# A two-layer graph convolution on one core: x loaded up front, row statistics on ScalarE, degree counting in pairs of edges, edge lists turned last

## The chip, the core and the metric

The kernel runs on one core of one Trainium2 chip. The core has five engines that run side by side, each through its own instruction list in order: PE (matrix products), DVE (VectorE), ACT (ScalarE), POOL (GpSimd) and SP (SyncE, which here only issues DMA transfers). Sixteen DMA engines move data between HBM and the on-chip memory SBUF. PE writes its products to PSUM, which DVE and ACT read. The metric is device time in microseconds (us) of one execution; the time of a kernel is the median of several runs.

## The reference

The input is x with 6250 nodes of 512 numbers, and 100000 edges (src, dst), sorted by dst. First each row of x is normalised and clipped at zero, then two Chebyshev graph convolutions run over it, with a layer norm and a leaky ReLU between them, and x is added at the end:

```python
h = jnp.maximum(_layernorm(x, axis=-1), 0.0)
deg = jax.ops.segment_sum(jnp.ones((src.shape[0],)), src, num_segments=n)
dinv = jnp.where(deg > 0, jax.lax.rsqrt(jnp.maximum(deg, 1.0)), 0.0)
norm = -dinv[src] * dinv[dst]
prop = lambda h: jax.ops.segment_sum(h[src] * norm[:, None], dst, num_segments=n)
h = h @ W1_0 + prop(h) @ W1_1 + b1
h = leaky_relu(layer_norm(h, gamma, beta))
out = x + h @ W2_0 + prop(h) @ W2_1 + b2
```

`deg` counts how often a node occurs in src. The factor `dinv[src]` can be put on the rows of a table before they are gathered, and `-dinv[dst]` on the sums.

## The kernel before

Nodes are cut into NB = 49 blocks of 128 (the last has 106), edges into NC = 782 chunks of 128. The kernel has a preparation and then `usual_path`, a loop over 2 layers by 49 blocks.

**Preparation** (`gnn_kernel`, L91 to L246), in the order of the code:

- Loads: `src_i`, the sources laid out 125 by 800 (L125); `dst_c` and `src_c`, the lists by chunks (L132 to L139), all on SP; four weight matrices and four vectors on ACT's queue (L142, L144). POOL makes number patterns (`diff`, `iota_r`), DVE makes the identity `ident` (L150).
- Turn of the edge lists (L157 to L169): PE transposes the 7 pieces of each list; the destinations stay in PSUM as `dl`, the sources are copied by ACT to `sidx`, the index list of the gathers.
- Degree count (L172 to L208): each source number is split into a low part (7 bits, `s_lo`) and a high part (`s_hi`, 0 to 48). In 50 rounds of GJ = 16 columns DVE compares the low parts with 0 to 127 (`lo`, L193) and the high parts with 0 to 48 (`hi`, L195), which gives one-hot rows in bf16; PE multiplies them, 16 products of 128 by 49 a round (L198), and sums them all in one PSUM tile `deg`. Then `dinv`, `ndinv` and `sdinv` are computed from it (L202 to L208).
- First table (L211 to L244): in 13 groups of GB = 4 blocks, three buffers deep, SP loads x (L219), DVE takes mean and variance of each row (L228, L229), ACT the square root (L231), DVE the scales (L234 to L238), ACT `relu(x*scale + bias)` with `dinv` multiplied in (L241), and SP stores the group to the table `tab[0]` in HBM (L243). The per-row scale and bias without `dinv` stay in `rs_all` and `nb_all` for the loop.

**The loop.** Each chunk's 128 source rows are fetched from the table by one indirect DMA on POOL (L272) into a ring of R = 44 buffers `zr`. The first gather waits for the whole table and for `sidx`. For each block DVE builds selection matrices `sel` (L324) from `dl`, PE multiplies them with the gathered rows (L335), in four strips of 32 output rows, ACT scales the sum to `agg` (L338), PE transposes it (L279) and multiplies it with one weight (L396). `own` (L283) loads the block's own rows of x again (L290), normalises them (L293), transposes them, and `start_products` (L302, its products at L304) multiplies them with the other weight. `finish` (L341) ends the block. PE and POOL follow the code's order exactly; the other engines are ordered by the scheduler. Memory of the preparation is given back at L246, and the loop's buffers take it over.

Of the kernel before, what the change touches and what calls it, by code (L numbers as in the profile page):

```python
# [8 lines left out]
F32 = mybir.dt.float32  # L9
BF = mybir.dt.bfloat16  # L10
I32 = mybir.dt.int32
AF = mybir.ActivationFunctionType
OP = mybir.AluOpType
# [5 lines left out]
P = 128  # L19
EPS = 1e-5  # L20
SLOPE = 0.01
# [7 lines left out]
def parts(r):  # L29

    return [(lo, hi) for lo, hi in ((0, r - r % 16), (r - r % 16, r)) if lo < hi]
# [16 lines left out]
def gnn_kernel(  # L48
# [27 lines left out]
    nc = tc.nc  # L76
    N, D = x.shape
    E = src.shape[0]
    NB = -(-N // P)
    EP = 125  # L80
    EJ = E // EP
# [7 lines left out]
    rows = [min(P, N - i * P) for i in range(NB)]  # L89
# [4 lines left out]
    def dup(ap, n):  # L94

        return bass.AP(tensor=ap.tensor, offset=ap.offset, ap=[[0, n], [1, ap.shape[0]]])

    tab = [dram.tile([NB * P, D], F32, name=f"tab{i}") for i in range(2)]
    h_tab = dram.tile([NB * P, D], F32, name="h_tab")

    ident = const.tile([P, P], F32, name="ident")
    iota_r = const.tile([P, P], F32, name="iota_r")
    ones = const.tile([P, P], F32, name="ones")
    eps = const.tile([P, 1], F32, name="eps")
    dinv = const.tile([P, NB], F32, name="dinv")
    ndinv = const.tile([P, NB], F32, name="ndinv")
    sdinv = const.tile([P, NB], F32, name="sdinv")
    rs_all = const.tile([P, NB], F32, name="rs_all")
    nb_all = const.tile([P, NB], F32, name="nb_all")
# [5 lines left out]
    n_seen = const.tile([P, NQ * NB], F32, name="n_seen")  # L115
# [6 lines left out]
    edges = ctx.enter_context(ExitStack())  # L122
    ep = edges.enter_context(tc.tile_pool(name="edges", bufs=1))
    src_i = ep.tile([EP, EJ], I32, name="src_i")
    nc.sync.dma_start(src_i, src.rearrange("(p j) -> p j", j=EJ))  # L125

    FG = NC // P - (E % (P * P) == 0)
    chunks = []
    for ids, fill, name in ((dst, NO_NODE, "dst_c"), (src, 0, "src_c")):
        t = ep.tile([P, NG, P], I32, name=name)  # L130
        nc.vector.memset(t[:, FG:, :], fill)
        nc.sync.dma_start(t[:, :FG, :], ids[: FG * P * P].rearrange("(g c e) -> c g e", c=P, e=P))  # L132
        whole = E // P - FG * P
        if whole:
            nc.sync.dma_start(t[:whole, FG, :],
                              ids[FG * P * P : (E // P) * P].rearrange("(c e) -> c e", e=P))
        if TAIL:
            nc.sync.dma_start(t[whole : whole + 1, FG, :TAIL],
                              ids[E - TAIL :].rearrange("(c e) -> c e", c=1))  # L139
        chunks.append(t)  # L140
    for t, w in zip(w_sb, (W1_1, W1_0, W2_1, W2_0)):
        nc.scalar.dma_start(t, w.rearrange("(k p) d -> p k d", p=P))  # L142
    for t, v in ((bias1, b1), (bias2, b2), (gam, gamma), (bet, beta)):
        nc.scalar.dma_start(t, dup(v, P))  # L144

    nc.gpsimd.iota(diff, pattern=[[1, P]], base=0, channel_multiplier=-1,
                   allow_small_or_imprecise_dtypes=True)
    nc.gpsimd.iota(iota_r, pattern=[[1, P]], base=0, channel_multiplier=0,
                   allow_small_or_imprecise_dtypes=True)
    nc.vector.tensor_single_scalar(ident, diff, 0.0, op=OP.is_equal)  # L150
    nc.vector.memset(ones, 1.0)
    nc.vector.memset(eps, EPS)

    nc.vector.memset(n_seen, 0.0)


    with tc.tile_pool(name="turn", bufs=1) as wp, tc.tile_pool(  # L157
        name="turn_ps", bufs=2, space=bass.MemoryType.PSUM
    ) as wps:
        for t, res in zip(chunks, (dl, sidx)):  # L160
            f = wp.tile([P, NG, P], F32, name="f", bufs=2)
            nc.vector.tensor_copy(f, t)
            for g in range(NG):
                if res is dl:
                    nc.tensor.transpose(dl[:, g * P : (g + 1) * P], f[:, g, :], ident)
                else:
                    fT = wps.tile([P, P], F32, name="fT")
                    nc.tensor.transpose(fT, f[:, g, :], ident)
                    nc.scalar.activation(sidx[:, g * P : (g + 1) * P], fT, AF.Copy)  # L169


    GJ = 16  # L172
    assert EJ % GJ == 0
    with tc.tile_pool(name="deg", bufs=1) as dp, tc.tile_pool(name="onehot", bufs=3) as ohp, tc.tile_pool(
        name="deg_ps", bufs=1, space=bass.MemoryType.PSUM
    ) as dps:
        iota_g = dp.tile([P, P, GJ], BF, name="iota_g")
        nc.gpsimd.iota(iota_g, pattern=[[1, P], [0, GJ]], base=0, channel_multiplier=0,
                       allow_small_or_imprecise_dtypes=True)
        half_i = dp.tile([EP, EJ], I32, name="half_i")  # L180
        s_lo = dp.tile([EP, EJ], BF, name="s_lo")
        s_hi = dp.tile([EP, EJ], BF, name="s_hi")
        nc.vector.tensor_single_scalar(half_i, src_i, P - 1, op=OP.bitwise_and)
        nc.vector.tensor_copy(s_lo, half_i)
        half_i2 = dp.tile([EP, EJ], I32, name="half_i2")
        nc.vector.tensor_single_scalar(half_i2, src_i, 7, op=OP.arith_shift_right)
        nc.vector.tensor_copy(s_hi, half_i2)
        deg = dps.tile([P, NB], F32, name="deg")
        for g in range(EJ // GJ):
            cols = slice(g * GJ, (g + 1) * GJ)  # L190
            lo = ohp.tile([EP, P, GJ], BF, name="lo")
            hi = ohp.tile([EP, NB, GJ], BF, name="hi")
            nc.vector.tensor_tensor(lo, s_lo[:, None, cols].to_broadcast([EP, P, GJ]),  # L193
                                    iota_g[:EP], op=OP.is_equal)
            nc.vector.tensor_tensor(hi, s_hi[:, None, cols].to_broadcast([EP, NB, GJ]),  # L195
                                    iota_g[:EP, :NB, :], op=OP.is_equal)
            for j in range(GJ):
                nc.tensor.matmul(deg, lo[:, :, j], hi[:, :, j], start=(g == 0 and j == 0),  # L198
                                 stop=(g == EJ // GJ - 1 and j == GJ - 1))
        root = dp.tile([P, NB], F32, name="root")  # L200
        some = dp.tile([P, NB], F32, name="some")
        nc.vector.tensor_scalar_max(root, deg, 1.0)  # L202
        nc.vector.tensor_single_scalar(some, deg, 0.0, op=OP.is_gt)
        nc.scalar.activation(root, root, AF.Sqrt)
        nc.vector.reciprocal(root, root)
        nc.vector.tensor_mul(dinv, root, some)
        nc.vector.tensor_scalar_mul(ndinv, dinv, -1.0)
        nc.vector.tensor_scalar_mul(sdinv, dinv, SLOPE)  # L208


    GB = 4  # L211
    with tc.tile_pool(name="t0", bufs=3) as pool:
        for i0 in range(0, NB, GB):
            g = [i for i in range(i0, min(NB, i0 + GB))]
            n = len(g)
            xt = pool.tile([P, GB, D], F32, name="xg")
            full = sum(rows[i] == P for i in g)
            if full:
                nc.sync.dma_start(xt[:, :full, :],  # L219
                                  x[i0 * P : (i0 + full) * P, :].rearrange("(i p) d -> p i d", p=P))  # L220
            if full < n:
                nc.vector.memset(xt[:, full:, :], 0.0)
                for lo, hi in parts(rows[g[-1]]):
                    nc.sync.dma_start(xt[lo:hi, full, :], x[g[-1] * P + lo : g[-1] * P + hi, :])
            st = pool.tile([P, GB, 6], F32, name="st")
            mv = pool.tile([P, GB, 2], F32, name="mv")
            for j in range(n):
                nc.vector.bn_stats(st[:, j, :], xt[:, j, :])  # L228
                nc.vector.bn_aggr(mv[:, j, :], st[:, j, :])  # L229
            sd = pool.tile([P, GB], F32, name="sd")  # L230
            nc.scalar.activation(sd[:, :n], mv[:, :n, 1], AF.Sqrt, bias=eps)  # L231
            rs = rs_all[:, i0 : i0 + n]
            nb = nb_all[:, i0 : i0 + n]
            nc.vector.reciprocal(rs, sd[:, :n])  # L234
            nc.vector.scalar_tensor_tensor(nb, mv[:, :n, 0], -1.0, rs, op0=OP.mult, op1=OP.mult)
            sc = pool.tile([P, 2, GB], F32, name="sc")
            nc.vector.tensor_mul(sc[:, 0, :n], rs, dinv[:, i0 : i0 + n])
            nc.vector.tensor_mul(sc[:, 1, :n], nb, dinv[:, i0 : i0 + n])  # L238
            t0 = pool.tile([P, GB, D], F32, name="t0")
            for j in range(n):  # L240
                nc.scalar.activation(t0[:, j, :], xt[:, j, :], AF.Relu, bias=sc[:, 1, j : j + 1],  # L241
                                     scale=sc[:, 0, j : j + 1])
            nc.sync.dma_start(tab[0][i0 * P : (i0 + n) * P, :].rearrange("(i p) d -> p i d", p=P),  # L243
                              t0[:, :n, :])  # L244

    edges.close()  # L246
    unseen = const.tile([1, 1], I32, name="unseen")
# [475 lines left out]
```

## Time and profile before

| what | us |
|---|---|
| median of 9 runs | 2750.56 |
| lowest and highest of them | 2728.08, 2762.71 |
| the profiled execution: its time, its span | 2739.88, 2738.0 |
| degree count, first compare to last product (L193 to L198) | 26.2 to 108.7 |
| loads of x for the table, first issue | 111.7 |
| last store to the table, issue | 193.1 |
| first gather | 197.5 |
| first and last `agg` of layer 1 | 271.7, 1493.4 |
| first gather, first `agg` of layer 2 | 1507.1, 1576.3 |

The profile's first part gives each engine's busy time, its share of the span, and its number of instructions:

```profile
PE 2148.9 (78%) x11848; PEld 817.0 (30%) x11848; DVE 653.8 (24%) x971; ACT 376.6 (14%) x672; POOL 1485.8 (54%) x1571
```

These shares are averages over stages that have nothing in common. In the first 200 us POOL gathers nothing, and from 127 to 201 us PE does little or nothing. A stage has to be read by itself, and for this the trace is cut into windows of time. A product of fp32 operands with 512 columns shows as two records on PE, so that 60 records of L335 are 30 products.

### The profile page before, as it was taken

Reading aid. Unit: us, or ns where it says so; the run is one execution under the profiler, and the core shown is the slowest. Engines: PE = TensorE matmul, PEld = TensorE weight load, DVE = VectorE, ACT = ScalarE, POOL = GpSimd, SP = SyncE. Lnnn points to the kernel's source line nnn. Section 1 sums busy time; section 2 is a strip of 40 time slices with the busy share of each in tenths; the row PEclk is TensorE's granted clock in tenths of the full one; section 3 lists DMA queues with packets and bytes.
Section 4 is the critical chain, followed back from the end, with each engine's and each line's share of the span. In section 5 each row is a group of like instructions: output and inputs, shape, how many; then the busy total and the mean of one; then the engine's idle time right before and its main releaser. Section 6 shows DMA issues by size and latency. Waiting matters only on the chain.

```text
span 2738.0 us, 29493 instructions
## 1 busy us (share of the span) xinstructions
PE 2148.9 (78%) x11848; PEld 817.0 (30%) x11848; DVE 653.8 (24%) x971; ACT 376.6 (14%) x672; POOL 1485.8 (54%) x1571
## 2 busy tenths in 40 slices
PE   6703888787878888787888388899888888879877
PEld 6600333232323322222333033332223222323332
DVE  7740322222222222222223011111111111111111
ACT  0240212111111212111222000000000000000000
POOL 0006666555555555645562666666666566555662
PEclk9955999999989999999999689999999999899999
DMA  3286676656666666756673667777776677666772
GB/s 103 99 310 186 207 211 197 192 170 196 190 182 180 185 196 181 207 155 187 191 209 123 195 198 214 206 211 212 210 208 206 185 211 211 190 184 200 214 212 89
DMA packets 184958, 521.13 MB, mean 190 GB/s; under 512 B 30379, under 2 KB 31941, under 8 KB 184810
## 3 DMA queue, kind: packets, MB, share of 16 engines
q0 software_dynamic: 125120, 410.09, 51.9%
q1 hardware_dynamic: 57002, 103.80, 11.2%
q10 hardware_dynamic: 2688, 5.24, 0.6%
q8 instruction: 95, 1.56, 0.2%
q14 instruction: 53, 0.43, 0.1%
HBM read 467.68 MB, written 51.34 MB: 190 GB/s over the span
## 4 chain that ended last, share of the span: by engine, by line
another core or an unknown queue 38%; PE 30%; DVE 12%; issue 9%; ACT 3%; DMA 0%; POOL 0%; ACTq 0%; DVEq 0%; SPq 0%; POOLq 0%
PE u_ps L396 13%; PE ps L335 10%; PE u_ps L304 4%; DVE sel L324 3%; PE aT_ps L279 2%; DVE aT L392 2%; DVE u_ps L358 1%; DVE u_ps L350 1%; DVE st L353 1%; DVE u_ps L360 1%; PE hT_ps L279 1%; DVE g L369 1%; ACT g L368 1%; ACT agg L338 1%
## 5 line engine op out<-in xcount | busy, mean ns | idle before, releaser
L272 POOL DMA_INDIRECT zr<-tab,sidx x1564 | 1482.7, 948 | 1184.7 <-PE ps L335 492.9
L335 PE MATMUL ps<-zr,sel 128*32 128x512 f32 x8680 | 1125.0, 597 | 148.5 <-DMA zr<-tab,sidx 89.6
L335 PEld LDWEIGHTS ps<-zr,sel 128*32 128x32 f32 x8680 | 319.5, 110 | 880.1 <-issue 833.5
L304 PE MATMUL u_ps<-w,hT 128*128 128x512 f32 x784 | 455.9, 710 | 17.0 <-issue 13.9
L396 PE MATMUL u_ps<-w,aT 128*128 128x512 f32 x784 | 398.6, 655 | 86.0 <-DVE aT L392 84.5
L324 DVE TENSOR_TENSOR sel<-dl,node 128x1536 f32<-128x1536 f32 (+5 forms) x110 | 160.9, 1472 | 1230.3 <-remote 1125.9
L279 PE MATMUL aT_ps<-ident,agg 128*128 128x128 f32 x392 | 78.4, 333 | 292.0 <-ACT agg L338 204.9
L396 PEld LDWEIGHTS u_ps<-w,aT 128*128 128x128 f32 x784 | 161.2, 213 | 344.2 <-issue 190.1
L338 ACT ACTIVATE agg<-ps,ndinv 128x512 f32<-128x512 f32 x98 | 67.4, 687 | 1302.9 <-remote 1173.5
L304 PEld LDWEIGHTS u_ps<-w,hT 128*128 128x128 f32 x784 | 157.3, 222 | 221.3 <-issue 217.6
L279 PEld LDWEIGHTS aT_ps<-ident,agg 128*128 128x128 f32 x392 | 50.2, 164 | 374.6 <-ACT agg L338 258.8
L297 ACT ACTIVATE hT<-hT_ps 128x512 f32<-128x512 f32 x98 | 58.5, 597 | 695.3 <-PE hT_ps L279 491.2
L392 DVE COPY aT<-aT_ps 128x512 f32<-128x512 f32 x98 | 67.8, 692 | 195.4 <-remote 148.0
L345 DVE TENSOR_TENSOR u_ps<-u_ps,bias 128x512 f32<-128x512 f32 x48 | 33.6, 700 | 253.4 <-PE u_ps L396 102.0
L350 DVE TENSOR_TENSOR u_ps<-u_ps,bias 128x512 f32<-128x512 f32 x49 | 34.3, 700 | 245.0 <-PE u_ps L396 190.8
L327 ACT ACTIVATE held<-sel 128x1536 bf16<-128x1536 f32 (+5 forms) x55 | 68.9, 1253 | 131.5 <-DVE sel L324 103.8
L198 PE MATMUL deg<-hi,lo 125*128 125x49 bf16 x800 | 80.7, 277 | 6.1 <-DVE hi L195 6.1
L198 PEld LDWEIGHTS <-lo 125*128 125x128 bf16 x800 | 79.4, 148 | 7.5 <-DVE hi L195 6.4
L279 PE MATMUL hT_ps<-ident,h 128*128 128x128 f32 x392 | 59.4, 274 | 13.3 <-ACT h L293 13.3
L279 PEld LDWEIGHTS hT_ps<-ident,h 128*128 128x128 f32 x392 | 49.2, 142 | 64.3 <-issue 50.8
L193 DVE TENSOR_TENSOR lo<-s_lo,iota_g 125x2048 bf16<-125x2048 bf16 x50 | 60.9, 1218 | 0.0
L365 DVE SCALAR_TENSOR_TENSOR t<-u_ps,dinv,t 128x512 f32<-128x512 f32 x49 | 36.8, 751 | 37.1 <-ACT t L364 25.0
(62 smaller groups left out, 492.0 us busy)
## 6 DMA issues: line engine op xcount, KB each, us to landing
zr<-tab,sidx POOLq DMA_INDIRECT x1564
xt<-in_x_dram SPq DMA_DIRECT2D x96, 256.0 KB
tab<-t SPq DMA_DIRECT2D x50, 256.0 KB
h_tab<-g SPq DMA_DIRECT2D x49, 256.0 KB
h<-h_tab SPq DMA_DIRECT2D x49, 256.0 KB
xg<-in_x_dram SPq DMA_DIRECT2D x12, 1024.0 KB
tab<-t SPq DMA_DIRECT2D x12, 1024.0 KB
out_dram<-o SPq DMA_DIRECT2D x48, 256.0 KB
```

Of the source, the lines that this page charges most:

```text
L193: nc.vector.tensor_tensor(lo, s_lo[:, None, cols].to_broadcast([EP, P, GJ]), iota_g[:EP], op=OP.is_equal)
L198: nc.tensor.matmul(deg, lo[:, :, j], hi[:, :, j], start=(g == 0 and j == 0), stop=(g == EJ // GJ - 1 and j == GJ - 1))
L272: nc.gpsimd.indirect_dma_start(out=zr[t % R], out_offset=None, in_=tab[layer], in_offset=bass.IndirectOffsetOnAxis(ap=sidx[:, t : t + 1], ...
L279: nc.tensor.transpose(ps[:, kc, :], h[:, kc * P : (kc + 1) * P], ident)
L304: nc.tensor.matmul(u_ps, hT[:, kc, :], w0[:, kc, :], start=(kc == 0), stop=False)
L324: nc.vector.tensor_tensor(o, d, i, op=OP.is_equal)
L327: nc.scalar.activation(held[:, : o.shape[1], : o.shape[2]] if len(o.shape) == 4 else held[:, 0, : o.shape[1], :], o, AF.Copy, accum_out=n_ ...
L335: nc.tensor.matmul(ps[q * Q : (q + 1) * Q, :], sel[:, q, s, :], zr[(lo + s) % R], start=(s == 0), stop=(lo + s == hi - 1))
L338: nc.scalar.activation(agg, ps, AF.Copy, scale=ndinv[:, b : b + 1])
L350: nc.vector.tensor_add(v, v, bias1)
L392: nc.vector.tensor_copy(aT, aT_ps)
L396: nc.tensor.matmul(u_ps, aT[:, kc, :], w1[:, kc, :], start=False, stop=(kc == KD - 1))
```

## The change

Only the preparation changes; `usual_path` is the same text.

- x is loaded whole, 12.8 MB, into SBUF tiles `xs`, in 8 groups of 2, 5, and then 7 blocks, on SP, right behind `src_i` and ahead of the edge lists, the weights and the vectors, which all move to SP behind it.
- ACT takes the row sums of the first 42 blocks (`Copy` with an accumulated output) and then the sums of squares about the mean (`Square`), one instruction of 512 columns per block and pass. DVE takes the last 7 blocks with its statistics instruction, after the count.
- The count splits a source into 6 low bits (LO = 64) and a high part (HI = 98). Two neighbouring edges lie interleaved in the innermost dimension: `lo` is 64 by 2, `hi` 98 by 2, and one product of 128 by 196 serves both edges. There are 20 rounds of GJ = 20 products, with two buffers in place of three. The product holds wanted counts (edge 0 with edge 0, 1 with 1) and unwanted ones; four small products with every second column of `ident` fold the wanted ones into `deg`.
- Scale and bias of all 49 blocks are then computed at once. The rows are scaled and clipped in place, the odd blocks by two DVE instructions, the even ones by ACT, and each group is stored when it is ready.
- The turn of the edge lists comes last.
- Some constants are filled by POOL in place of DVE.

```diff
+    groups, i = [], 0
+    while i < NB:
+        n = min(NB - i, 2 if not groups else 5 if len(groups) == 1 else 7)
+        groups.append((i, n))
+        i += n
...
+            nc.sync.dma_start(t[:, :full, :],
+                              x[i0 * P : (i0 + full) * P, :].rearrange("(i p) d -> p i d", p=P))
...
-        nc.scalar.dma_start(t, w.rearrange("(k p) d -> p k d", p=P))
+        nc.sync.dma_start(t, w.rearrange("(k p) d -> p k d", p=P))
...
+    for (i0, n), t in zip(groups[:-1], xs):
+        for j in range(n):
+            junk = ep.tile([P, D], BF, name="junk", bufs=2)
+            nc.scalar.activation(junk, t[:, j, :], AF.Copy, accum_out=sums[:, i0 + j : i0 + j + 1])
+        nc.scalar.activation(nm_all[:, i0 : i0 + n], sums[:, i0 : i0 + n], AF.Copy, scale=-1.0 / D)
+        for j in range(n):
+            junk = ep.tile([P, D], BF, name="junk", bufs=2)
+            nc.scalar.activation(junk, t[:, j, :], AF.Square, bias=nm_all[:, i0 + j : i0 + j + 1],
+                                 accum_out=sq_all[:, i0 + j : i0 + j + 1])
...
+        for g in range(EJ // (2 * GJ)):
+            hot = []
+            for s, n, name in ((s_lo, LO, "lo"), (s_hi, HI, "hi")):
+                t = ohp.tile([EP, GJ, n, 2], BF, name=name)
+                nc.vector.tensor_tensor(
+                    t, s[:, g * 2 * GJ : (g + 1) * 2 * GJ].rearrange("p (j s) -> p j s", s=2)[:, :, None, :]
+                    .to_broadcast([EP, GJ, n, 2]),
+                    iota_g[:EP, None, :n, :].to_broadcast([EP, GJ, n, 2]), op=OP.is_equal)
+                hot.append(t.rearrange("p j n s -> p j (n s)"))
+            for j in range(GJ):
+                nc.tensor.matmul(both_ps, hot[0][:, j, :], hot[1][:, j, :], start=(g == 0 and j == 0),
+                                 stop=(g == EJ // (2 * GJ) - 1 and j == GJ - 1))
+        nc.vector.tensor_copy(both, both_ps.rearrange("p (b t s) -> p b t s", t=2, s=2))
...
+        for t in range(2):
+            for i in range(2):
+                nc.tensor.matmul(deg[t * LO : (t + 1) * LO, :], each[:, i, :], both[:, :, t, i],
+                                 start=(i == 0), stop=(i == 1))
...
+                if i % 2:
+                    nc.vector.tensor_scalar(t[:, j, :], t[:, j, :], sc[:, 0, i : i + 1], sc[:, 1, i : i + 1],
+                                            op0=OP.mult, op1=OP.add)
+                    nc.vector.tensor_scalar_max(t[:, j, :], t[:, j, :], 0.0)
+                else:
+                    nc.scalar.activation(t[:, j, :], t[:, j, :], AF.Relu, bias=sc[:, 1, i : i + 1],
+                                         scale=sc[:, 0, i : i + 1])
+            nc.sync.dma_start(tab[0][i0 * P : (i0 + n) * P, :].rearrange("(i p) d -> p i d", p=P), t)
...
-    GJ = 16
...
-            nc.vector.tensor_tensor(lo, s_lo[:, None, cols].to_broadcast([EP, P, GJ]),
-                                    iota_g[:EP], op=OP.is_equal)
...
-    GB = 4
-    with tc.tile_pool(name="t0", bufs=3) as pool:
...
-                nc.vector.bn_stats(st[:, j, :], xt[:, j, :])
-                nc.vector.bn_aggr(mv[:, j, :], st[:, j, :])
...
-                nc.scalar.activation(t0[:, j, :], xt[:, j, :], AF.Relu, bias=sc[:, 1, j : j + 1],
-                                     scale=sc[:, 0, j : j + 1])
-            nc.sync.dma_start(tab[0][i0 * P : (i0 + n) * P, :].rearrange("(i p) d -> p i d", p=P),
-                              t0[:, :n, :])
```

In the changed instruction lists, the lists of edges are turned on DVE, PE and ACT behind the last scaling; the first instructions of the loop on DVE (`sel`), ACT (`node`) and SP (`xt`) wait for the table's stores, because their buffers lie where `xs` lay. In the kernel before, the first `sel` ran at 20 us and block 0's own products at 125 us.

## The prediction

> **What bounds the kernel now.** I read the windows of time first, then the timeline of the first 200 us, then the waits. The question is which time ends the preparation, because the loop behind it is the same in both kernels. The waits of POOL give it:
>
> ```profile
> POOL zr L272 <- DMA xt<-in_x_dram: 173.1, 1, 173.1
> 197.47 1.10 POOL L272 DMA_INDIRECT zr<-tab,sidx  x1 [173.12 <-DMA xt<-in_x_dram]
> ```
>
> POOL stands still for 173.1 us until the first gather at 197.47. (The load of xt named there came last by chance; the gather reads the whole table.) Whatever makes this start earlier by a microsecond takes a microsecond off the end, as long as the loop runs as before. The 197 us are two stages in series. In the first, about 22 to 109 us, DVE and PE count and DMA is idle; in the second, 112 to 197, x is loaded, normalised and stored and PE is idle. Windows of time show it (columns: us; busy us of PE, weight loads, DVE, ACT, POOL; clock; DMA share; GB/s):
>
> ```profile
> 50.00:100.00 50.00, 50.00 (x498) 49.22 (x497) 50.00 (x63) 0.00 (x0) 0.00 (x0) 1.00 0.01 1
> 150.00:200.00 50.00, 0.00 (x0) 0.00 (x0) 25.16 (x91) 24.40 (x39) 2.05 (x2) 0.50 0.87 308
> ```
>
> In the first row DVE has no gap and DMA moves 1 GB/s; in the second DMA moves 308 GB/s and PE does nothing. The change lays the load and the statistics beside the count. No byte is saved: x is still read once here and twice in the loop.
>
> **The count.** Groups of the profile, with shapes kept apart:
>
> ```profile
> L193 DVE TENSOR_TENSOR lo<-s_lo,iota_g 125x2048 bf16<-125x2048 bf16 x50 | 60.9, 1218 | 0.0
> L195 DVE TENSOR_TENSOR hi<-s_hi,iota_g 125x784 bf16<-125x784 bf16 x50 | 27.9, 558 | 0.0
> L198 PE MATMUL deg<-hi,lo 125*128 125x49 bf16 x800 | 80.7, 277 | 6.1 <-DVE hi L195 6.1
> ```
>
> DVE never waits here. Starts in the timeline are 26.16 (lo), 27.29 (hi), 27.77 (lo): 1.13 us from lo to hi and 0.48 from hi to lo, so (1.13 - 0.48)/(2048 - 784) = 0.52 ns an element and about 0.07 us an instruction. 50 rounds of 1.61 us are 80.6 us. A new round compares 20 x 64 x 2 + 20 x 98 x 2 = 6480 elements: 3.37 + 0.14 = 3.51, say 3.53 us; 20 rounds take 70.6. That is 10 us less, if the rate holds.
>
> It is not certain to hold, since the new innermost run is two bf16, one word of 4 bytes, which `s_lo` repeats 64 times and `s_hi` 98 times. [...] But the trace has a repeated word already, in fp32:
>
> ```profile
> L324 DVE TENSOR_TENSOR sel<-dl,node 128x1536 f32<-128x1536 f32 x66 | 116.0, 1758 | 807.4 <-remote 723.7 <-PE ps L335 83.7
> L324 DVE TENSOR_TENSOR sel<-dl,node 128x1024 f32<-128x1024 f32 x8 | 9.8, 1224 | 194.5 <-remote 193.6 <-PE ps L335 0.9
> ```
>
> `sel` reads each word of `dl` 32 times in a row and costs (1758 - 1224)/512 = 1.04 ns an element, twice the 0.52 above. So repeating a word isn't dear, and I take 3.53. The other end is the fp32 rate, should packing in pairs be lost: 6480 x 1.04 + 0.14 = 6.9 us, 138 us. No gain below 3.5 is open, as nothing in the trace runs two-tensor operations faster.
>
> PE has 3.53 us for 20 products, 176 ns each. After the last compare (106.87) the last 16 old products were done by 108.65, so at most 111 ns each with 49 columns. No product of bf16 with 196 columns is shown. L304 moves 512 columns of fp32 in 0.43 us a record, so 196 columns of bf16 should add between 0 and 0.43 x 147/512 = 0.12 us; added to 111 ns that makes 111 to 234. I take 150, hidden behind DVE. At 234 PE would be the bound and add 20 x 20 x 0.058 = 23 us.
>
> The start moves too. Before, `half_i` ran at 21.85, behind the turn of the lists, and took 2.93 us beside POOL's pattern of 2048 columns (2.47 us). Now `src_i` is first on SP, the pattern has 196 columns, and the turn comes later. The first lists landed at 14.9 us behind 4 MB of weights; `src_i` alone should land by 6 (4 to 8). Four conversions of about 0.5 us: first compare at 8.2, last at 78.8, last product 2.7 later at 81.5.
>
> **Load and statistics, beside the count.** Full windows of before move 390 to 409 GB/s while loading and 310 to 340 while loading and storing. 12.8 MB at 350 take 37 us; x is in SBUF by 45, the rest (some 6 MB) by 62. SP queues weights and vectors behind x; their first reader is the loop. ACT: 84 instructions of 512 columns. `held` of L327 is the nearest row: 405 ns for 256 columns and 1058 for 1024, so 623 for 512, and in the timeline its accumulator read overlaps so far that the distance of starts is 0.40. With a per-row bias add some 0.1 (L293's 803 against 597 for L368 is 0.2 for two pointers). 42 x (0.62 + 0.72) = 56, seven small steps and their waits 4, start at 6: ACT is done at about 66, under the count's 82. It would matter only beyond 0.19 us more for each instruction.
>
> **From count to scales.** Copy of the counts 0.35, four folding products 1.5, DVE's statistics (7 x 0.67 + 7 x 0.17, partly after the count, and between these steps in the new order), root, reciprocals and small products at 0.13 to 0.47 each, as in L202 to L208: 5.5 us, scales at 87. Before, 108.65 to 111.7 was 3.1 for this.
>
> **Scaling and stores.** ACT 25 x 0.73 (L241's distance of starts) = 18 us; DVE 24 x 2 x 0.33 = 16 by the pace of the conversions (800 columns in 0.48, less the fixed part), up to 0.8 a block with waits, 19. Seven blocks every 2.8 us beat the stores: 7 x 0.26 MB at 350 GB/s are 5.2. So DMA sets the pace: first store issued at 88, 12.8 MB at 350 = 36.7, and 2 us to land: 127. No window of before stores alone. At 400 it is 32, at 300 it is 43, so minus 5 or plus 6. The turn of the lists (two casts of 0.63, 14 transposes in 4.3 by L165 and L168, 7 copies) starts behind the last scaling at about 107 and ends by 115, under the stores. Without that cover it would cost 8.
>
> First gather 127.3 in place of 197.5: **70 us**.
>
> **The loop's start.** `node`, `sel`, `xt`, `h` of blocks 0 and 1 now wait for the stores. From there: load 3.3, L293 0.8, transposes 1.1, copy behind ACT's queue 1.5, eight records of L304 at 0.85 (as at 125 us) 6.8, transposes 1.1: PE is free for L335 after 14.6 us. Chunks arrive one in 1.25 us and the fourth product needs chunk 10, at 16.6 before. The three products ahead of it no longer run early: 3 us late, bounds 0 and 8.
>
> Both layers open with a slow stretch: 74.2 us from first gather to first `agg` in layer 1, 69.2 in layer 2, although block 0's last chunk is there after some 25.
>
> ```profile
> 220.00:230.00 10.00, 5.46 (x24) 1.00 (x16) 0.00 (x0) 0.00 (x0) 7.58 (x8) 0.98 0.74 209
> 230.00:240.00 10.00, 4.05 (x4) 1.12 (x5) 0.00 (x0) 0.00 (x0) 7.59 (x8) 0.50 0.72 208
> 240.00:250.00 10.00, 2.02 (x2) 0.29 (x1) 0.00 (x0) 0.00 (x0) 7.58 (x8) 0.50 0.74 211
> ```
>
> The clock is full in the first row and falls back to half in the next. [...] By the rows, PE stays slow until the unbroken run of gathers ends (POOL first stalls at 258.7), and in layer 2 PE had worked until 5.6 us before and was as slow. I take the rows: 74 again.
>
> **Sum.** 197.5 - 127.3 - 3 = 67. The profiled execution took 2739.9 (span 2738.0 and 1.9 around it), 10.7 under the median of the nine; the saving is the same number of microseconds on either: 2739.9 - 67 = 2673, and for the median 2750.6 - 67 = 2683.
>
> **Rivals.**
>
> [...]
> 2. *Packing in pairs lost*, the slower side. Place: DVE's compare; price 6.9 us a round or more. It decides from (197.5 - 127.3 - 3)/20 + 3.53 = 6.9 us on: 2750 just there, and 2770 if single words cost 1.2 ns an element (7.9 a round). For it: no row shows a run of two. Against: both operands and the output stay bf16 with step one. 9%, half of it slower by more than half a per cent.
> 3. *Block 0's own products fall into the slow stretch*: records on PE are 2.8 us apart at 235 to 244, so eight of L304 and four transposes could cost 20 to 35 us rather than 9; 2705. For it, they now run after gathers start; against, they have no gathered operand, and whatever is left runs quickly once gathers stop. 9%.
> [...]
> 5. PE as the bound of the count: 2706, inside the range. 4%.
>
> **Numbers.** The forecast, 2683, has 60%; its own range is 2665 to 2705, from the store rate, the landing of `src_i`, and the spread of medians. To hold 8 in 10 the range takes in rivals 3 and 5 and most of 1 and 4: 2635 to 2730. A change of 0.5%, 14 us, is about what can be told from none. Faster by more: forecast, 1 (2727 lies under 2737), 3, 4, 5, less their tails: 0.87. Within: 0.08. Slower: 0.05.
>
> **What would show it.** First gather near 127 (above 140 the count or stores were mispriced); lo and hi together 3.5 us a round with no wait of DVE on PE; ACT's `junk` done before the count; a store window above 330 GB/s with no gap; `sidx` done before the last store; first `agg` about 77 us after the first gather. The forecast is wrong if the compare runs at 1 ns an element, or if that last distance changes by tens of microseconds.

## The result, and the profile after

| | before | after |
|---|---|---|
| median, us (runs) | 2753.48 (31) | 2688.86 (10) |
| lowest and highest, us | 2717.73, 2805.41 | 2652.76, 2721.84 |
| profiled execution: time, span | 2739.88, 2738.0 | 2694.29, 2692.5 |
| first gather, us | 197.47 | 124.89 |
| first `agg` of layer 1, counted from it | 74.2 | 69.9 |

The changed kernel is faster: the ratio of the times is 0.9726, with a 95% interval of 0.9684 to 0.9769. On 2753 us that is 75 us (64 to 87); the medians differ by 64.6. The medians count every run; the ratio leaves out those more than 1.5% above the fastest of their kernel, and the profiled execution of the changed kernel is one of these.

In the one profiled execution of each kernel the first gather is 72.6 us earlier, and the end only 45.5 us (2738.0 - 2692.5). The loop is the same text; in this execution its second layer took 1168.4 us from the first to the last `agg` against 1145.7 before. The loop's own spread is of this size (single runs of one kernel lie up to 88 us apart), so the first gather, which came at 124.9 to 125.3 us in every trace of a kernel that leaves the preparation alone, is the exact measure for a change of the preparation, and the ratio of many runs the measure for the whole.

POOL's wait and the first gather, from the waits and from the timeline of the changed kernel:

```profile
POOL zr L315 <- DVE sel L367: 121.3, 1, 121.3
```

```profile
124.89 1.10 POOL L315 DMA_INDIRECT zr<-tab,sidx  x1 [121.32 <-DVE sel L367]
```

173.1 us of waiting have become 121.3. (The name of the releaser is again chance: `sel` was released by the last store as well.)

The timeline of DVE at the end of the count (start, us, engine, line, operation, shapes):

```profile
72.73 1.49 DVE L215 TENSOR_TENSOR lo<-s_lo,iota_g 125x2560 bf16<-125x2560 bf16 x1
74.13 2.20 DVE L215 TENSOR_TENSOR hi<-s_hi,iota_g 125x3920 bf16<-125x3920 bf16 x1
76.24 1.49 DVE L215 TENSOR_TENSOR lo<-s_lo,iota_g 125x2560 bf16<-125x2560 bf16 x1
77.64 2.20 DVE L215 TENSOR_TENSOR hi<-s_hi,iota_g 125x3920 bf16<-125x3920 bf16 x1
79.75 1.28 DVE L229 BATCH_NORM_STATS2 st<-xs 128x6 f32<-128x512 f32 x2
```

A round lasts 76.24 - 72.73 = 3.51 us, and no idle time stands behind any of these lines. The groups of the first 124 us, with shapes kept apart (busy us, mean ns | idle before):

```profile
L221 PE MATMUL both_ps<-hi,lo 125*128 125x196 bf16 x400 | 39.1, 254 | 42.7 <-DVE hi L215 42.6
...
L194 ACT ACTIVATE junk<-xs,nm_all 128x512 bf16<-128x512 f32 x42 | 29.7, 709 | 0.2
L215 DVE TENSOR_TENSOR lo<-s_lo,iota_g 125x2560 bf16<-125x2560 bf16 x20 | 29.7, 1485 | 0.0
L190 ACT ACTIVATE junk<-xs 128x512 bf16<-128x512 f32 x42 | 25.8, 613 | 6.9 <-DMA xs<-in_x_dram 6.9
```

PE now waits for DVE for 42.7 us; DVE waits for nobody; ACT's statistics wait 6.9 us for x, nearly all of it for its first group. One round of PE:

```profile
76.38 1.86 PE L221 MATMUL both_ps<-hi,lo 125*128 125x196 bf16 x20 [1.65 <-DVE hi L215]
```

The windows show the new overlap (us; busy us of PE, weight loads, DVE, ACT, POOL; clock; DMA share; GB/s):

```profile
10.00:50.00 40.00, 22.19 (x220) 20.41 (x221) 40.00 (x25) 39.38 (x120) 0.00 (x0) 1.00 1.01 350
50.00:80.00 30.00, 15.16 (x164) 13.82 (x162) 30.00 (x18) 18.33 (x53) 0.00 (x0) 1.00 0.30 101
...
90.00:120.00 30.00, 4.03 (x14) 2.69 (x14) 16.96 (x43) 16.28 (x28) 0.00 (x0) 0.50 1.02 376
```

From 10 to 50 us DVE, ACT and DMA are all full at once. The last row is the stage that is left: stores at 376 GB/s, and DMA at full share.

### The profile page after: what moved, and what is told of

Same layout as the page of the kernel before. It is cut to its first block, busy times and chain, and to the rows that moved or that the text cites. A ratio compares the mean times of both kernels' runs of the same rounds, so it can differ in the third digit from the quotient of the medians.

```text
span 2692.5 us, 28647 instructions
## 1 busy us (share of the span) xinstructions
PE 2127.7 (79%) x11456; PEld 787.3 (29%) x11456; DVE 622.7 (23%) x824; ACT 413.7 (15%) x811; POOL 1485.5 (55%) x1577
## 4 chain that ended last, share of the span: by engine, by line
another core or an unknown queue 42%; PE 29%; DVE 14%; issue 11%; ACT 3%; DMA 1%; ACTq 0%; DVEq 0%
PE u_ps L439 13%; PE ps L378 10%; PE u_ps L347 4%; DVE sel L367 3%; PE aT_ps L322 2%; DVE aT L435 2%; DVE lo L215 1%; DVE u_ps L401 1%; DVE u_ps L393 1%; DVE st L396 1%; ACT agg L381 1%; DVE u_ps L403 1%; PE hT_ps L322 1%; ACT t L407 1%
## 5 line engine op out<-in xcount | busy, mean ns | idle before, releaser
L378 PE MATMUL ps<-zr,sel 128*32 128x512 f32 x8680 | 1137.6, 598 | 89.3 <-issue 60.3
L378 PEld LDWEIGHTS ps<-zr,sel 128*32 128x32 f32 x8680 | 326.7, 110 | 825.7 <-issue 792.2
L439 PE MATMUL u_ps<-w,aT 128*128 128x512 f32 x784 | 407.6, 668 | 92.7 <-DVE aT L435 88.9
L347 PE MATMUL u_ps<-w,hT 128*128 128x512 f32 x784 | 454.1, 708 | 15.4 <-issue 12.6
L221 PE MATMUL both_ps<-hi,lo 125*128 125x196 bf16 x400 | 39.1, 254 | 42.7 <-DVE hi L215 42.6
L322 PE MATMUL hT_ps<-ident,h 128*128 128x128 f32 x392 | 59.4, 274 | 16.6 <-ACT node L354 16.6
L221 PEld LDWEIGHTS <-lo 125*128 125x128 bf16 x400 | 35.7, 100 | 45.8 <-issue 34.6
L215 DVE TENSOR_TENSOR hi<-s_hi,iota_g 125x3920 bf16<-125x3920 bf16 x20 | 43.9, 2195 | 0.0
```

The costliest lines, as they stand in the source:

```text
L215: nc.vector.tensor_tensor(t, s[:, g * 2 * GJ : (g + 1) * 2 * GJ].rearrange("p (j s) -> p j s", s=2)[:, :, None, :] .to_broadcast([EP, GJ, ...
L221: nc.tensor.matmul(both_ps, hot[0][:, j, :], hot[1][:, j, :], start=(g == 0 and j == 0), stop=(g == EJ // (2 * GJ) - 1 and j == GJ - 1))
L322: nc.tensor.transpose(ps[:, kc, :], h[:, kc * P : (kc + 1) * P], ident)
L347: nc.tensor.matmul(u_ps, hT[:, kc, :], w0[:, kc, :], start=(kc == 0), stop=False)
L378: nc.tensor.matmul(ps[q * Q : (q + 1) * Q, :], sel[:, q, s, :], zr[(lo + s) % R], start=(s == 0), stop=(lo + s == hi - 1))
L439: nc.tensor.matmul(u_ps, aT[:, kc, :], w1[:, kc, :], start=False, stop=(kc == KD - 1))
```

## The experiments

### Four parts of the change, taken back one at a time

The vector engine sets the preparation up to the scales, and DMA from there: that is the theory. Each kernel here is the changed one with one part undone. What it costs shows at the first gather; the times themselves, four to ten runs each beside thirteen of the kernel before (2662.75 us), have intervals of 0.4 to 1.4% to either side, and only the last of the four is told from the change by its time. Not taken back by themselves were the scales of all blocks at once, the scaling shared by DVE and ACT, and the place of the weights behind x.

**The old count** (7 low bits, one edge per product):

```diff
-    LO = P // 2
-    HI = 2 * NB
-    GJ = 20
+    GJ = 16
...
-                nc.tensor.matmul(both_ps, hot[0][:, j, :], hot[1][:, j, :], start=(g == 0 and j == 0),
+                nc.tensor.matmul(both_ps, lo[:, :, j], hi[:, :, j], start=(g == 0 and j == 0),
```

> The changed kernel with one part undone: the degree count in the old layout (128 low values by 16 edges and 49 high values by 16 edges a round, 50 rounds, three buffers, one product per edge column, no folding). Loads, statistics, stores and the turn stay as changed. Theory (the vector engine's compares set the length of the count stage): the old round cost 1.60 us for 16 columns, 50 rounds are 80 us, where the interleaved count took 20 x 3.51 = 70.2 us; less the folding (about 0.5 us), so the first gather goes from 124.9 to about 134 to 135 us and the time rises by about 9 to 10 us. Rival (the load of x or the statistics on the scalar engine, done at about 68 us, set the stage): no change, first gather within 2 us of 124.9.

First gather 136.16: 11.3 us later than 124.89. The ratio to before is 0.9785 (0.9661 to 0.9909). DVE's timeline in this kernel:

```profile
87.24 1.22 DVE L213 TENSOR_TENSOR lo<-s_lo,iota_g 125x2048 bf16<-125x2048 bf16 x1
88.38 0.56 DVE L215 TENSOR_TENSOR hi<-s_hi,iota_g 125x784 bf16<-125x784 bf16 x1
88.85 1.22 DVE L213 TENSOR_TENSOR lo<-s_lo,iota_g 125x2048 bf16<-125x2048 bf16 x1
```

A round of 16 columns takes 88.85 - 87.24 = 1.61 us, also beside the load and ACT's statistics, and DVE leaves the count at 90.47, 10.7 us later than at 79.75. The count itself, from first compare to last, is 10.3 us longer (80.7 for 70.4); `src_i` landed 0.4 us later here. The compare sets this stage; the rival is out.

**All statistics on DVE:**

```diff
-            nc.scalar.activation(junk, t[:, j, :], AF.Copy, accum_out=sums[:, i0 + j : i0 + j + 1])
...
+            nc.vector.bn_stats(st[:, i0 + j, :], t[:, j, :])
+            nc.vector.bn_aggr(mv[:, i0 + j, :], st[:, i0 + j, :])
```

> The changed kernel with one part undone: the statistics of all 49 blocks on the vector engine after the count, none on the scalar engine. Theory (the vector engine is the one busy engine up to the scales, so work put on it is paid in full): 42 more blocks at about 0.66 us for their two instructions are +28 us, first gather at about 153 us, time +28 us. Rival (the scalar engine's statistics are no shorter than the path, or the vector engine has slack while data come): first gather within 5 us of 124.9.

First gather 154.59, 29.7 us later; ratio 0.9785 (0.9662 to 0.9908). In the groups of its first 156 us:

```profile
L218 DVE BATCH_NORM_STATS2 st<-xs 128x6 f32<-128x512 f32 x49 | 31.9, 656 | 0.0
```

49 blocks without a wait: DVE pays for all of them. In the kernel before, the same work lay under the load and the store of the table, where DVE was busy for 25 of 50 us (150 to 200); what it cost there was not tested. It had to be moved once the load lay beside a count that keeps DVE full.

**Edge lists loaded and turned first:**

The two loops that load `dst_c` and `src_c` move up to stand ahead of the load of x, and the lines below, with the transposes under them, ahead of the count:

```diff
+    nc.vector.tensor_single_scalar(ident, diff, 0.0, op=OP.is_equal)
+    with tc.tile_pool(name="turn", bufs=1) as wp, tc.tile_pool(
...
+            f = wp.tile([P, NG, P], F32, name="f", bufs=2)
+            nc.vector.tensor_copy(f, t)
```

> The changed kernel with one part undone: the edge lists are loaded ahead of x and turned ahead of the count, as before; all else as changed. Theory: the vector engine waits for the two lists, makes the identity and the two conversions to float in front of the count, and the lists' slow loads hold x back: +4 to +8 us at the first gather (129 to 133). Rival (the turn lay hidden before as well, so that its place is worth nothing): first gather within 2 us of 124.9.

First gather 133.41, 8.5 us later; ratio 0.9727 (0.9584 to 0.987), too wide to tell 8 us. DVE's timeline:

```profile
9.16 0.63 DVE L191 CAST f<-dst_c 128x896 f32<-128x896 int32 x1 [9.16 <-DMA dst_c<-in_dst_dram]
10.39 0.63 DVE L191 CAST f<-src_c 128x896 f32<-128x896 int32 x1 [0.60 <-DMA src_c<-in_src_dram]
10.94 0.22 DVE L185 TENSOR_SCALAR ident<-diff 128x128 f32<-128x128 f32 x1
15.89 0.58 DVE L221 TENSOR_SCALAR half_i<-src_i 125x800 int32<-125x800 int32 x1 [4.74 <-PE fT L197]
```

DVE's start on `half_i` goes from 7.42 to 15.89. About 3.7 of these 8.5 us are the lists, casts and identity (11.16 against 7.42), and 4.7 are a wait for the last transposes, which the count's tiles have to wait for here (they come after the turn's buffers are given back). So the place of the turn is worth what stands between DVE and the count, and more than half of it is a wait for memory rather than work. That it is the memory is read from the code; the trace shows only that the last transposes end the wait.

**x loaded after the count** (each load waits for one small copy from the finished counts):

```diff
+        nc.vector.tensor_copy(t[:, 0, 0:1], both[:, 0, 0, 0:1])
+        if full:
+            nc.sync.dma_start(t[:, :full, :],
+                              x[i0 * P : (i0 + full) * P, :].rearrange("(i p) d -> p i d", p=P))
```

> The changed kernel with its overlap taken away: x is loaded only after the count is done, and the scalar engine's statistics follow the loads. Everything else is as changed, x is still read once. Theory (most of the gain is that load and statistics lie beside the count): the load of 25.7 MB at 387 GB/s is 66 us at most and the statistics trail it by a few us, or are the longer at about 42 x 1.31 = 55 us, so the scales come 60 to 70 us later: first gather at about 185 to 195 us, that is, about where it was before the change (197.5). Rival (the gain comes from reading x once, whenever that is): at most 20 us later, first gather below 145 us.

First gather 184.90, 60.0 us later, and only 12.6 before the kernel before; ratio 0.99 (0.9858 to 0.9942). The 25.7 MB of the expectation is twice what x has (12.8 MB), so its term of 66 us for the load was wrong; the load took about 35 us (issued at 82.6, no more traffic from about 117), and the other term, the statistics, carried the delay. Windows:

```profile
100.00:110.00 10.00, 0.00 (x0) 0.00 (x0) 0.00 (x0) 9.94 (x32) 0.00 (x0) 0.50 1.04 387
...
130.00:140.00 10.00, 0.00 (x0) 0.00 (x0) 0.00 (x0) 9.94 (x31) 0.00 (x0) 0.50 0.00 0
...
160.00:170.00 10.00, 3.20 (x13) 2.44 (x13) 6.97 (x18) 5.53 (x11) 0.00 (x0) 0.50 1.04 380
```

First load and ACT together, then ACT for a good 27 us without any load (DVE's seven blocks took some 5 us of these), then the stores. ACT's statistics, from 86.37 to about 145, are, with the load under them, what the count hides in the changed kernel. The stage behind the count even takes longer here than in the kernel before (from the first load's issue, 184.9 - 82.6 = 102 us against 197.5 - 111.7 = 86), because before it was pipelined by groups. Most of the gain is the place beside the count: without it 12.6 of the 72.6 us are left.

The four costs, 11.3, 29.7, 8.5 and 60.0, add up to 109.5 us where the change brought 72.6. They may: each was taken from the changed kernel, where the other parts leave its work no cover.

### The slow stretch at the start of each layer

The prediction had to carry a stretch that it couldn't explain: some 70 us from the first gather to the first `agg`, although block 0's data are there after 25. In the changed kernel it is there again, though PE worked right up to it. Windows:

```profile
155.00:165.00 10.00, 4.04 (x4) 0.51 (x4) 0.00 (x0) 0.00 (x0) 7.58 (x8) 0.50 0.76 211
165.00:175.00 10.00, 3.80 (x4) 0.39 (x3) 0.00 (x0) 0.00 (x0) 7.58 (x8) 0.50 0.71 211
...
185.00:195.00 10.00, 3.04 (x3) 0.57 (x2) 0.19 (x1) 0.24 (x1) 1.82 (x2) 0.50 0.23 72
```

PE starts four records in 10 us, 2.8 us apart, while POOL issues eight gathers; POOL's train ends with the gather at 183.93, and `agg` follows at 194.76.

The records of PE are not the whole of the delay. The last one of block 0's sum starts at 180.53 and ends at 181.54, so that `agg`, which waits for this sum, starts 13.2 us after it (37.7 in the kernel before). In the median of all 98 blocks this gap is 3.9 us in the changed kernel, but 0.1 us in the kernel with most gathers left out and 0.1 us on the quick chip of the next section. What ended the waits of `agg`, in the changed kernel here and then on that chip (total us, times, longest):

```profile
180.53 1.01 PE L378 MATMUL ps<-zr,sel 128*32 128x512 f32 x1 [1.79 <-issue]
```

```profile
ACT agg L381 <- remote: 1153.9, 82, 70.7
```

```profile
ACT agg L381 <- PE ps L378: 936.1, 98, 27.6
```

"remote" means that no instruction in the profile ends when the signal comes. So what comes late may be PE's work (the ends of products are modelled) or the signal of its end; no run tells them apart, and "held up" below stands for both.

Theory A said that PE is held up as long as gathers run without a gap; rival B that the pace is PE's own. The edits:

```diff
-    R = 44
+    R = 32
```

(and 54 in the second kernel); in the third, a gap of POOL's behind block 0's chunks:

```diff
+                if b == 0:
+                    ahead = max(hi for _, hi in ranges[0])
+                elif b == 1:
+                    nc.gpsimd.tensor_copy(held_back[:, layer : layer + 1], agg[:, 0:1])
```

and in the fourth, most gathers left out:

```diff
-                    gather(layer, t)
+                    if t < R:
+                        gather(layer, t)
```

> The changed kernel with one size changed: the ring of gathered chunks has 32 buffers instead of 44, so that the first unbroken train of gathers in a layer is 12 gathers (15 us at 1.253 us) shorter. It bears on the 70 us from a layer's first gather to its first aggregate, which every kernel so far shows. Theory A (the tensor engine hardly gets on while gathers are issued without a gap, and is released some 10 us after the ring is full): first aggregate 55 us after the first gather, in both layers. Rival B (the pace is the tensor engine's own, at its lower clock or in its first columns, whatever the gathers do): 69 to 70 us as before. The time of the whole may go either way: the shorter ring makes gathers wait more in the steady loop.

> The changed kernel with one size changed: the ring of gathered chunks has 54 buffers instead of 44, so that the first unbroken train is 10 gathers (12.5 us) longer. Theory A (the tensor engine waits for a gap in the gathers): first aggregate 82 us after the first gather, in both layers. Rival B (the tensor engine's own pace): 69 to 70 us. The whole: +25 us by A from the two starts, if the steady loop does not gain from the deeper ring.

> The changed kernel with a gap put into the gathers: in each layer only the chunks of block 0 are gathered (about 20), then the gathering engine waits for block 0's aggregate (a copy of one column of it on that engine) before it gathers on. Theory A: first aggregate 33 to 38 us after the first gather instead of 70, second one at about 75 instead of 95; so up to 20 us a layer, 40 us in all, off the time. Rival B: first aggregate at 69 to 70 us still, and the gathers held back for all of that time: about +35 us a layer, 70 us slower.

> The changed kernel without most of its gathers: only the first 44 of each layer are made, the others are left out, and the products use what lies in the ring, so the output is not the reference's. What it shows is the loop of the other engines alone. Theory A: first aggregate at about 65 to 70 us as before (the train of 44 is still there), then blocks at the tensor engine's own pace, 16 to 19 us each instead of 25, since they no longer lose time to gathers. Rival B: the blocks go at 25 us as before, so that the gathers are hidden in the loop and the tensor engine sets it.

| kernel | last gather of the first train | first `agg` after first gather | after the train's last gather | first gather to last `agg` of layer 2 | ratio to before (interval) |
|---|---|---|---|---|---|
| ring of 32 | 167.91 | 52.4 | 9.8 | 2551.2 | 0.9695 (0.9575 to 0.9815) |
| ring of 44, the change | 183.93 | 69.9 | 10.8 | 2552.0 | 0.9726 (0.9684 to 0.9769) |
| ring of 54 | 196.73 | 83.3 | 11.9 | 2556.3 | 0.9815 (0.9738 to 0.9892) |
| gathers held after block 0 | 146.45 | 28.4 | 6.9 | 2560.7 | 0.9852 (0.9781 to 0.9923) |

The first aggregate moves with the end of the train, at 9.8 to 11.9 us behind it, and with a train of 18 gathers it comes after 28, 6.9 us behind it. Layer 2 shows the same: 52.5, 69.2, 86.7 and 27.0 us. Theory A holds in these runs (the kernel before took 2768.55 us beside them); B, which wanted 69 to 70 each time, is out. In the kernel with held gathers the stretch comes back with the next train (timeline of ACT and POOL):

```profile
153.37 0.69 ACT L382 ACTIVATE agg<-ps,ndinv 128x512 f32<-128x512 f32 x1 [15.06 <-PE ps L379]
154.12 0.18 POOL L425 COPY held_back<-agg 128x1 f32<-128x1 f32 x1 [6.73 <-ACT agg L382]
...
218.63 0.69 ACT L382 ACTIVATE agg<-ps,ndinv 128x512 f32<-128x512 f32 x1 [52.32 <-remote]
```

The second `agg` needs 65.3 us after the first; together 93.6, where the change has 69.9 + 24.8 = 94.7. So the hoped-for 20 us a layer did not come. Nor did the ring's length matter in the end: the column of whole loops differs by 9.5 us at most, one execution each, and the intervals of the three rings overlap. That of the held gathers begins just above the end of the change's, so that this kernel is, if anything, the slower one. Part of what the short ring saves at the start of a layer it pays at its end: the last four blocks of layer 1 took 79 us with 32 buffers and 70 with 44. No kernel here is shown to be faster than the change.

With the gathers after the first 44 of each layer left out, the first `agg` comes after 62.3 us, a little below the 65 to 70 of the expectation, and the next ones follow every 17.7 us in the mean of a layer instead of every 25.6 and 24.3 (time 1977.41, one run):

```profile
203.46 0.69 ACT L381 ACTIVATE agg<-ps,ndinv 128x512 f32<-128x512 f32 x1 [2.06 <-PE ps L378]
218.43 0.69 ACT L381 ACTIVATE agg<-ps,ndinv 128x512 f32<-128x512 f32 x1 [2.09 <-PE ps L378]
```

So gathers slow PE in the whole loop, not only at its start; its waits for gathered rows, as the changed kernel's profile has them, are only 18.3 us in all.

### Half the bytes, and the changed kernel on other chips

```diff
-                out=zr[t % R], out_offset=None, in_=tab[layer],
+                out=zr[t % R][:, : D // 2], out_offset=None, in_=tab[layer].rearrange("n (h d) -> (n h) d", h=2),
```

> The changed kernel with the gathers cut to half the bytes: each brings 256 of the 512 columns into a chunk (rows of the first half of the table, seen as rows of half the length), the other half of each chunk is set to zero once; the number of gathers, their order and their waits are as changed, and the output is not the reference's. The ring-size runs have shown that the tensor engine hardly gets on while gathers run without a gap; this asks whether it is the bytes that do it. Theory D (the bytes in flight: the 16 DMA engines, or what lies behind them): with half the bytes, at the same 1.253 us a gather, first aggregate 30 to 45 us after the first gather instead of 70. Rival P (the issuing of the gathers, 128 rows each, whatever their size): 69 to 70 us again, and blocks of 24 to 25 us.

First `agg` 25.3 us after the first gather, blocks every 20.0 us, 2122.0 us: just what theory D wanted. But the run fell on another chip (number 14, where all experiments so far ran on 13), and there the kernel before took 2199.92 us. So the changed kernel and the half-row kernel were run side by side. They came to a third chip, number 12, which is as quick.

> The changed kernel itself, unedited, beside the half-row kernel and the kernel before in one session: where the half-row kernel ran first, the kernel before took 2200 us instead of 2660 to 2770, so that its fast start cannot be laid to the bytes without this. If the place is one of the slow kind (before at 2650 us or more): first aggregate 70 us after the first gather, blocks of 24 to 25 us. If it is of the fast kind (before near 2200 us): first aggregate at about 25 to 30 us, blocks of 20 us, time about 2125 us, that is 73 us less than before there too, since the part ahead of the first gather has come out alike in every run.

> The half-row kernel again, unedited (each gather brings 256 of 512 columns, the output is not the reference's), in the same session as the changed kernel. Theory D (bytes in flight hold the tensor engine up): in a place where the changed kernel needs 70 us to its first aggregate, this one needs 25 to 45 us and its blocks take 20 us. Rival (the place alone did it): in such a place it needs 69 to 70 us too. In a place of the fast kind nothing tells them apart.

The changed kernel, unedited, took 2127.77 us (2123.3 to 2128.63, 4 runs) against 2201.06 (2198.07 to 2202.53, 7 runs) of before: ratio 0.9669 (0.9652 to 0.9685), 73.3 us. Its first gather is at 125.15, its first `agg` 26.3 us later, its blocks 20.0 us. The half-row kernel took 2126.56, with 25.3 and 20.0. On this chip there is nothing for half the bytes to mend, and the changed kernel needs no half rows for the fast start; on chip 14 it was not run itself. Windows of the changed kernel on chip 12, to be laid beside the same two windows above:

```profile
155.00:165.00 10.00, 7.91 (x40) 2.58 (x42) 4.45 (x8) 2.76 (x5) 7.56 (x8) 1.00 0.78 232
165.00:175.00 10.00, 7.73 (x50) 2.05 (x43) 1.65 (x2) 1.26 (x2) 7.55 (x8) 1.00 0.85 266
```

The same eight gathers in 10 us, at the same or a higher rate of bytes (232 and 266 GB/s for 211 and 211), and PE starts 40 and 50 records beside them instead of 4.

> The half-row kernel a third time (each gather brings 256 of 512 columns, the output is not the reference's), because its first two runs fell in a place where the changed kernel does not have the slow start either. If the kernel before takes 2650 us or more beside it: theory D (bytes in flight) has first aggregate at 25 to 45 us after the first gather and blocks of 20 us; the rival (the place, or the issuing of gathers whatever their size) has 69 to 70 us and blocks of 24 to 25 us. If the kernel before is near 2200 us again, the question stays open.

2123.91 us, with 2198.7 for the kernel before beside it, on chip 11: a quick chip for the third time, and no answer. What holds PE up beside gathers elsewhere stays open. That the recording of the profile has a part in it isn't excluded either.

## Why the prediction was right

It said 2683, by a saving of 67 us; the median is 2688.86, 64.6 under that of before. That these lie only 2.4 us apart is in part luck: the ratio gives 75 us with 64 to 87, and the steps below, put right, give more than 67. On chip 12, where the loop is steady, the saving is 73.3 us, within a microsecond of the 72.6 by which the first gather moved in the traces taken elsewhere (the kernel before has no trace on a quick chip). So what is saved ahead of the first gather reaches the end undiminished, as the sum assumed. Step by step:

- **The compare.** 3.53 us a round were taken, and 3.51 were measured. The rate came from the old compares, and that a repeated word keeps it, from `sel`, by likeness only: `sel` reads its repeated fp32 word from PSUM, `lo` and `hi` read pairs of bf16 from SBUF. That it carried over is a little luck. By the starts in DVE's timeline above `lo` takes 1.40 us and `hi` 2.11, so (2.11 - 1.40)/(3920 - 2560) = 0.52 ns an element, as before: no loss for a word repeated 64 or 98 times. Rival 2 (6.9 us a round or more) is out, and no run shows the slower round that the 2727 of the chances would need.
- **PE.** 150 ns a product were taken from a range of 111 to 234; 20 products took 1.86 us, 93 ns each, below the range: its low end, 111, was itself an "at most". It didn't matter, since DVE set the pace at 93 as at 150, and rival 5 is out.
- **The start.** `half_i` began at 7.42 for an assumed 6, so the count ended a microsecond later than worked out (last compare 79.8 for 78.8).
- **ACT.** Done with the statistics at 67.2 for 66, and 17 us ahead of the scales' first need of it at 84.8.
- **Scales and stores.** The first scaling started at 86.8 for 87, the first store went at 88.2 for 88. Then a term that was off: 350 GB/s and 127 us for the end of the stores; they ran at 376, and the loop's first load went at 123.99. First gather 124.9 for 127.3.
- **The turn of the lists** (105.8 to 111.3) lay wholly under the stores, as was said.
- **The loop's start.** 3 us were added to the 74 of before; it was 69.9, and 69.0 to 69.7 in the four kernels with a part taken back, which have the same ring. PE was free for the sums 10.6 us after the first gather for 14.6, and its fourth product of them set out 17.3 us after it, for 16.6 before; so at most 0.7 of the 3 us was real. Why the kernel before took 4 us more than all the others stays open. Rival 3 is out: the eight records of block 0's own products took 5.4 us, ahead of the stretch.

```profile
129.73 5.40 PE L347 MATMUL u_ps<-w,hT 128*128 128x512 f32 x8 [1.09 <-ACT hT L340]
```

The stretch did not vanish either, though PE came to it at a full clock. The mean granted clock was 0.84 in the 10 us before the first of the windows above:

```profile
145.00:155.00 10.00, 6.17 (x32) 1.43 (x25) 0.00 (x0) 0.00 (x0) 7.59 (x8) 0.84 0.73 209
```

So PE had the full clock for most of this window. Within it, from 149.74 on, its records came one by one all the same, and the clock was at a half only afterwards (0.87 in the mean of 150 to 155 us, 0.50 from 155 on). The step was right to take the rows of before. They did not tell that on chip 12 the first `agg` comes 26.3 us after the first gather. Since the saving there, 73.3 us, is what the first gather gained elsewhere (72.6) and hardly more, the kernel before must have the short start on that chip too. No run shows a saving that goes 48 us beyond the forecast, to the 2635 at which the range begins: the first `agg` came 69.9 us after the first gather for 74.2 before.

The errors, 2.4 us at the first gather and about 7 at the loop's start, both lay on the careful side. Without them the sum gives 72.6 + 4.3 = 76.9 us, close to the 75 of the ratio; the interval of 64 to 87 covers both sums.

## What to carry to other kernels

When two stages in series use different engines, work out which engine is full in each, and lay the one beside the other; then count again what each engine has to do in the joint stage, since work that was hidden before (here 30 us of statistics on DVE) is paid in full once its engine becomes the one that sets the pace. Judge a change of a preparation at a milestone that repeats to half a microsecond, and use the whole time only as the check that the gain arrives. Before a kernel's fast run is laid to its edit, look at what the unedited kernel took beside it: here the place alone made 20% of the time.

## What the runs showed of the hardware

Where the kernel before takes 2660 to 2770 us, PE is held up by an unbroken train of gathers, to about one record in 2.8 us, and runs freely some 10 us after it; on three others (11, 12 and 14), where it takes 2200, with the same 1.25 us a gather, it isn't; the changed kernel was traced on 12 alone of these. Nor is it the chip alone: two sets of runs on chip 13 gave 2662.75 and 2768.55 us for the kernel before. In the changed kernel's first stretch the starts of PE's records, from 149.74 to 189.64 us, lie 1.4, 2.1, 2.8 or 3.5 us apart, all multiples of 0.70; what has this period isn't known. POOL's waits for PE over the whole kernel, from the waits of the changed kernel in the slow place and on chip 12 (total us, times, longest):

```profile
POOL zr L315 <- PE ps L378: 514.5, 269, 11.3
```

```profile
POOL zr L315 <- PE ps L378: 65.2, 214, 0.3
```

On chip 12 a block takes 20.0 us, which is 16 gathers of 1.25 us: there the issue of gathers sets the loop, and elsewhere a block takes longer than its gathers (25.6 and 24.3 us in the two layers). The mean granted clock was 0.978 there and 0.91 here, but the clock is not the cause of the 2.8 us: from 142 to 146 us, at a granted clock of 0.50, PE still started four records every 0.85 us.

Loads of x ran at 386 to 387 GB/s and stores at 364 to 384 GB/s in full windows of 10 us (the changed kernel and the one with x late). DVE's round of the count took 3.51 us beside the load (9.37 to 12.88) as after it (72.73 to 76.24).
